# Another written-out order for a 128-row linear layer on one core: rounding before the sum, loads in parts

## The chip, the cores and the metric

One core of a Trainium2 chip runs the kernel. The metric is device time in microseconds (us): the median of the kernel's runs, here 107.94 us from three runs (107.92 to 108.06). A profile of one execution of the kernel before is at hand.

## The reference

```python
x: (4, 1024, 512)   cond_512: (4, 256)   W: (1536, 512)   b: (512,)
hidden = concatenate([cond_512, cond_512], axis=-1)            # (4, 512)
x_mean = mean(x, axis=1, keepdims=True)                        # (4, 1, 512)
fused  = concatenate([x, x_mean * ones, hidden * ones], -1)    # (4, 1024, 1536)
out    = x + relu(einsum('bld,do->blo', fused, W) + b)
```

All in float32. W has three blocks of 512 rows: one for x itself, one for the mean of x over the 1024 places of a batch row, one for `hidden`. The last two give one vector of 512 numbers for each of the four batch rows, called the bias here.

## The kernel before, in words

The output has 32 tiles of 128 places (eight for a batch row), each 128x512. For each tile the core computes x·W by TensorE. To keep float32 accuracy with fast products, x and W are split into a rounded part (`hi`, `w_hi`) and a remainder (`lo`, `w_lo`); a tile needs for each of four blocks j of 128 inputs the three products hi·w_hi, lo·w_hi and hi·w_lo: twelve matmuls of 128x128 by 128x512.

x must be turned (inputs on the partitions) before it can be a stationary operand. The first eight tiles are turned by TensorE (`turn`, L414: four transposes into one PSUM tile `xT`); the other 24 by VectorE from a second, differently laid out load of x called `z` (L416). Tiles 0 to 3 are turned one by one ("whole" pieces: one tile, all four j; pieces 0 to 3), later ones four tiles at a time ("units", one piece for each j: pieces 4 to 7 are tiles 4 to 7, pieces 8 to 11 tiles 8 to 11, and so on). Each piece is rounded by ScalarE (`hi`, L427), and the remainder is taken by VectorE or GpSimd (`lo`, L443). For whole pieces VectorE also sums over the places (`sum`, L436, tile `sums`); in the others ScalarE's accumulator does that. `hi`, `sum` and the VectorE `lo` of a piece read the same PSUM tile, and the program lets a second engine read it only when the first is through, in the order in which they were emitted.

W is split likewise: `w_hi` by ScalarE (L394) or VectorE (L396), `w_lo` by VectorE or GpSimd (L399).

The bias of a row is a chain: GpSimd adds the two halves of the third block of W (`add_cond`, L458, from `w_cond`), ScalarE scales by the condition (`weigh`, L462), GpSimd sums (`term`, L467), ScalarE starts an accumulator (`acc_start`, L478), VectorE adds the mean's four terms (`mean`, L481, from `total` and `scaled`, L471 and L474, and from `w_mean`), then `upper` (ScalarE L487), `fold` (VectorE L491), `rows_hi` (ScalarE L494), `rows_lo` (VectorE L497), one matmul `pb` (TensorE L501) and its copy `bias` (ScalarE L505).

An output tile's PSUM bank is emptied by `freed`: copied by ScalarE (L545) for the first ten tiles, which wait in SBUF for their bias (`biased`, GpSimd L550); added to the bias by VectorE (L547) for others; or, where the bias was put into the bank first (`preload`, ScalarE L517), finished by VectorE in one step (L543). Then come `relu` (ScalarE L553), `finished` (GpSimd L556, adds x) and `stored` (a DMA from SP, L561). Five PSUM banks serve the output tiles, so tile t needs `freed` of tile t-5. There are 13 SBUF output buffers, five of 1 MB for loads of x and W, three for z.

Nothing is left to a scheduler: `make_plan` lists the tasks, and `ORDER`, a string of numbers found offline, says in which order they are emitted. A number's half is the index of the task in `make_plan`, its last bit picks the first or the second engine the task allows. Each engine runs its tasks in that order and waits at each for what it needs; so does SP's queue for the DMA issues. The costs in `make_plan` (MB, ZMB, START and the pairs of numbers) reach the program in one way only: while TensorE would be idle in the first 12 us by these costs, warming matmuls (`fill`, L335) are put in.

Of the kernel before, what the change touches and what calls it, by code (L numbers as in the profile page):

```python
# [8 lines left out]
F32 = mybir.dt.float32  # L9
# [13 lines left out]
HALF = D // 2  # L23
G = 4
S_BUFS, O_BANKS, Z_BUFS, X_BUFS, O_BUFS, N_WARM = 14, 5, 3, 5, 13, 5
BY_PE = (0,1,2,3,4)
PARK = set(range(10))
BIAS_FIRST = {14,15,20,21,22,23,28,29,30,31}
FINE = 4
EXTRA = ()  # L30
XS_BUFS = 4
WARM_TO = 12.0

UNITS = [(0, k, 1) for k in range(4)] + [(0, 4, G)]
# [30 lines left out]
class Plan:  # L65
    HAND = 0.06
    ISSUE, LAND = 1.0, 0.7
    START = {"pe": 3.3, "sp": 0.75, "act": 2.3, "dve": 1.3, "pool": 3.5}

    def __init__(self):  # L70
        self.tasks = {}
# [23 lines left out]
SP = {"sp": (0.42, 0.42)}  # L95
ZQ = {"sp": (0.42, 0.42)}
MB = 2.62
ZMB = 5.4
MM = 0.2335
STEP = 3 * MM  # L100


def x_here(t):
    return ("x", 0, t) if t < G else ("x", t // G, 0)


def due(t, j, n=0, h=0):
    return 6.5 + (t * J + j) * STEP + n * MM + (h or 0) * J * STEP / 2


def make_plan():
    plan = Plan()
    loads = [
        (("x", 0, 0), MB / 4), (("w", 0), MB / 4 + 1.6), (("w", 1), MB / 4), (("x", 0, 1), MB / 4),
        (("w", 2), MB / 4), (("w", 3), MB / 4), (("x", 0, 2), MB / 4), (("x", 0, 3), MB / 4)
    ]
    chain = []
    for key, cost in loads:
        plan.add(key, SP, [], pipe=cost, soft=chain)
        chain = [key]  # L120
    plan.add(("c",), {"act": (0.42, 2.3)}, [], due=-9.0)
    first = chain
    for key in (("w_cond",), ("w_mean",)):
        plan.add(key, SP, [], pipe=MB, soft=first)
    plan.add(("b",), SP, [], pipe=0.05, soft=[("w_cond",)])
    chain = first
    for n, u in enumerate(BY_Z):
        for i in range(NQ):
            deps = []
            if n >= Z_BUFS:  # L130
                deps = [("turn", c) for c in range(len(PIECES)) if PIECES[c][0] == BY_Z[n - Z_BUFS]]
            late = [("hi", 1)] if "act" in ZQ and not n else []
            if "act" in ZQ and n:
                deps.append(("z", BY_Z[n - 1], i))
            plan.add(("z", u, i), ZQ, deps, pipe=ZMB / 4, soft=chain + late)
            chain = [("z", u, i)]
    x_slots = [0, "w", "cond"] + list(range(1, NT // G))
    if 4 in BY_PE:
        x_slots = [0, "w", 1, "cond"] + list(range(2, NT // G))
    chain = first  # L140
    for n, g in enumerate(x_slots):
        if g in (0, "w", "cond"):
            continue
        deps = []
        if n >= X_BUFS:
            v = x_slots[n - X_BUFS]
            deps = ([("w_hi", j) for j in range(J)] + [("w_lo", j) for j in range(J)] if v == "w" else
                    [("add_cond", k) for k in range(KH)] if v == "cond" else
                    [d for i in range(G) for d in x_read(v * G + i)])
        plan.add(("x", g, 0), SP, deps, pipe=MB, soft=chain + ([("w_cond",)] if n > x_slots.index("cond") else []))  # L150
        chain = [("x", g, 0)]
    for j in range(J):
        plan.add(("w_hi", j), {"act": (0.54, 0.63), "dve": (0.35, 0.43)}, [("w", j)])
        plan.add(("w_lo", j), {"dve": (0.61, 0.69), "pool": (1.3, 1.35)}, [("w_hi", j)])

    kinds = {True: [], False: []}
    for c, (u, js) in enumerate(PIECES):
        r, k0, n = UNITS[u]
        whole = len(js) > 1
        deps = ([x_here(t) for t in range(FIRST_TILE[u], FIRST_TILE[u] + n)]  # L160
                if u in BY_PE else [("z", u, i) for i in range(NQ)])
        same = kinds[in_sbuf(c)]
        n_bufs = XS_BUFS if in_sbuf(c) else 2
        if len(same) >= n_bufs:
            deps.append(("lo", same[-n_bufs]))
            if len(PIECES[same[-n_bufs]][1]) > 1:
# [46 lines left out]
    for t in range(NT):  # L213
        r, k = divmod(t, NK)
# [23 lines left out]
    for t in range(NT):  # L238
# [18 lines left out]
        else:  # L257
# [32 lines left out]
def kernel(  # L290
# [67 lines left out]
    def load_x(e, g, i):  # L358
        r, k = divmod(g * G, NK)
        if not i:  # L360
            xs[g] = xpool.tile([P, G, D], F32, tag="x", name=f"x{g}")
        n = 1 if not g else G
        nc.sync.dma_start(out=xs[g][:, i : i + n], in_=xv[r, :, k + i : k + i + n, :])

    def load_z(e, u, i):
# [11 lines left out]
            w_src["x"] = xpool.tile([P, J, D], F32, tag="x", name="w_x")  # L377
        nc.sync.dma_start(out=w_src["x"][:, j, :], in_=Wv[0, :, j])

    def load_cond(e):  # L380
        w_src["cond"] = xpool.tile([P, 2, KH, D], F32, tag="x", name="w_cond")
        nc.sync.dma_start(
            out=w_src["cond"], in_=W[2 * D : 3 * D].rearrange("(s h p) o -> p s h o", p=P, h=KH)
        )

    def load_mean(e):
# [223 lines left out]
```

## Time and profile before

| | |
|---|---|
| median of three runs | 107.94 us (107.92 to 108.06) |
| the profiled execution's own time | 107.55 us |
| its span, first to last instruction | 105.7 us |
| TensorE clock granted | 1.000 |
| PE busy | 100.5 us (95%) |
| VectorE, ScalarE, GpSimd busy | 74.5, 60.1, 71.4 us |
| bytes moved | 26.31 MB, mean 249 GB/s |

All engines' rows are in us from the span's start. PE is TensorE's matmuls, PEld its weight loads, DVE is VectorE, ACT ScalarE, POOL GpSimd, SPq the queue that issues the DMAs. A row's bracket gives how long the engine sat idle before the instruction, and what ended that. Matmuls are pipelined: a row of one matmul shows 0.40 us, though the next begins about 0.23 us after it, so the distance of starts is what counts.

### The profile page before, as it was taken

Reading aid. Unit: us, or ns where it says so; the run is one execution under the profiler, and the core shown is the slowest. Engines: PE = TensorE matmul, PEld = TensorE weight load, DVE = VectorE, ACT = ScalarE, POOL = GpSimd, SP = SyncE. Lnnn points to the kernel's source line nnn. Section 1 sums busy time; section 2 is a strip of 40 time slices with the busy share of each in tenths; the row PEclk is TensorE's granted clock in tenths of the full one; section 3 lists DMA queues with packets and bytes.
Section 4 is the critical chain, followed back from the end, with each engine's and each line's share of the span. In section 5 each row is a group of like instructions: output and inputs, shape, how many; then the busy total and the mean of one; then the engine's idle time right before and its main releaser. Section 6 shows DMA issues by size and latency. Waiting matters only on the chain.

```text
span 105.7 us, 1434 instructions
## 1 busy us (share of the span) xinstructions
PE 100.5 (95%) x448; PEld 78.9 (75%) x448; DVE 74.5 (70%) x109; ACT 60.1 (57%) x134; POOL 71.4 (68%) x64
## 2 busy tenths in 40 slices
PE   5979999999999999999999999999999999999970
PEld 2446877888888788888788788687888888888860
DVE  1287256248999999797999999999989620920160
ACT  5014075997895997779988507799930402970000
POOL 6005080959327499999999999998999980468000
PEclk9999999999999999999999999999999999999999
DMA  2699999999999999999999999318999999727252
GB/s 76 195 370 387 395 418 229 189 199 199 200 199 200 260 177 199 201 201 300 404 397 234 179 243 385 137 58 217 387 411 338 360 260 249 298 109 297 100 207 91
DMA packets 22961, 26.31 MB, mean 249 GB/s; under 512 B 1189, under 2 KB 13737, under 8 KB 22826
## 3 DMA queue, kind: packets, MB, share of 16 engines
q1 hardware_dynamic: 22946, 26.22, 93.0%
q8 instruction: 3, 0.05, 0.2%
q14 instruction: 4, 0.03, 0.1%
q10 hardware_dynamic: 8, 0.00, 0.0%
HBM read 17.83 MB, written 8.39 MB: 248 GB/s over the span
## 4 chain that ended last, share of the span: by engine, by line
PE 93%; DVE 2%; ACT 1%; issue 0%
PE po_None L529 83%; PE xT L414 4%; PE po L529 3%; PE pw L335 2%; PE pb L501 1%; DVE sums L436 1%; DVE lo L443 1%; ACT hi L427 1%; DVE o L543 0%; DVE w_hi L396 0%; DVE warm L323 0%; PE pt L450 0%; DVE one L325 0%
## 5 line engine op out<-in xcount | busy, mean ns | idle before, releaser
L529 PE MATMUL po_None<-w_hi,hi 128*128 128x512 f32 x124 | 48.6, 400 | 0.6 <-DVE w_hi L396 0.6
L529 PE MATMUL po_None<-w_hi,lo 128*128 128x512 f32 x124 | 48.0, 397 | 0.0
L529 PE MATMUL po_None<-w_lo,hi 128*128 128x512 f32 x124 | 47.9, 398 | 0.0
L556 POOL TENSOR_TENSOR o<-o,x 128x512 f32<-128x512 f32 x22 | 27.9, 1300 | 5.6 <-issue 4.5
L529 PEld LDWEIGHTS po_None<-w_hi,hi 128*128 128x128 f32 x124 | 23.2, 188 | 7.2 <-issue 1.1
L529 PEld LDWEIGHTS po_None<-w_lo,hi 128*128 128x128 f32 x124 | 23.2, 188 | 5.7 <-POOL w_lo L399 0.4
L529 PEld LDWEIGHTS po_None<-w_hi,lo 128*128 128x128 f32 x124 | 23.2, 189 | 5.0
L416 DVE STREAM_TRANSPOSE xT<-z 128x512 f32<-128x512 f32 x24 | 25.3, 1094 | 0.1
L427 ACT ACTIVATE hi<-xT 128x512 fp32r<-128x512 f32 x32 | 19.3, 608 | 10.6 <-PE xT L414 5.9
L443 POOL TENSOR_TENSOR lo<-xT,hi 128x512 fp32r<-128x512 f32 x12 | 15.5, 1298 | 4.5 <-ACT hi L427 4.3
L443 DVE TENSOR_TENSOR lo<-xT,hi 128x512 fp32r<-128x512 f32 x20 | 13.4, 683 | 5.2 <-ACT hi L427 5.2
L550 POOL TENSOR_TENSOR o<-o,bias 128x512 f32<-128x512 f32 x10 | 12.9, 1301 | 1.9 <-ACT bias L505 1.9
L553 ACT ACTIVATE o<-o 128x512 f32<-128x512 f32 x22 | 13.1, 622 | 1.3 <-POOL o L550 0.9
L481 DVE SCALAR_TENSOR_TENSOR acc<-w_mean,tot,acc 128x512 f32<-128x512 f32 x16 | 12.1, 753 | 0.9 <-ACT tot L474 0.5
L547 DVE TENSOR_TENSOR o<-po_None,bias 128x512 f32<-128x512 f32 x12 | 7.7, 678 | 5.7 <-ACT bias L505 5.1
L543 DVE SCALAR_TENSOR_TENSOR o<-po_None,x 128x512 f32<-128x512 f32 x9 | 6.1, 687 | 7.3 <-PE po_None L529 7.3
L487 ACT ACTIVATE upper<-acc 64x512 f32<-64x512 f32 x4 | 2.4, 598 | 8.4 <-DVE acc L481 8.4
L467 POOL TENSOR_TENSOR cond<-b_sb,term 128x512 f32<-128x512 f32 x4 | 5.2, 1290 | 2.9 <-ACT term L462 2.9
L436 DVE TENSOR_REDUCE sums<-xT 128x4 f32<-128x512 f32 x4 | 2.7, 691 | 6.2 <-PE xT L414 3.2
L545 ACT ACTIVATE o<-po_None 128x512 f32<-128x512 f32 x10 | 5.5, 602 | 1.6 <-PE po_None L529 1.5
L399 POOL TENSOR_TENSOR w_lo<-w_x,w_hi 128x512 fp32r<-128x512 f32 x1 | 1.6, 1553 | 6.7 <-ACT w_hi L394 6.7
L414 PEld LDWEIGHTS xT<-ident,x 128*128 128x128 f32 x32 | 4.8, 208 | 1.7 <-issue 1.4
(45 smaller groups left out, 72.4 us busy)
## 6 DMA issues: line engine op xcount, KB each, us to landing
out_dram<-o SPq DMA_DIRECT2D x31, 256.0 KB, 4.6
x<-in_x_dram SPq DMA_DIRECT2D x7, 1024.0 KB, 8.6
z<-in_x_dram SPq DMA_DIRECT2D x24, 256.0 KB, 9.3
x<-in_x_dram SPq DMA_DIRECT2D x4, 256.0 KB, 5.7
w_x<-in_L_cond_W_dram SPq DMA_DIRECT2D x4, 256.0 KB, 5.4
w_cond<-in_L_cond_W_dram SPq DMA_DIRECT2D x1, 1024.0 KB, 7.8
w_mean<-in_L_cond_W_dram SPq DMA_DIRECT2D x1, 1024.0 KB, 12.1
out_dram<-o SPq DMA_DIRECT2D x2, 128.0 KB, 2.0
```

The lines of the kernel that those rows point to most:

```text
L414: nc.tensor.transpose(v[:, (m * n + i) * P : (m * n + i + 1) * P], x_t[:, j], ident)
L416: nc.vector.transpose(v[:, : n * P].rearrange("p (n t) -> p n t", t=Q), zs[u].rearrange("p n (a j) -> p n j a", j=J)[:, : n * NQ, js[0], :],)
L427: nc.scalar.activation(hi[c][:, :m], xT[c][:, :m], AF.Copy, accum_out=sums[:, r, js[0], s : s + 1] if len(js) == 1 else None,)
L443: eng[e].tensor_tensor(lo[c][:, :m], xT[c][:, :m], hi[c][:, :m].bitcast(F32), ALU.subtract)
L481: nc.vector.scalar_tensor_tensor(acc[r], w_mean[:, j, :], totals[r][:, j : j + 1], acc[r], ALU.mult, ALU.add)
L529: nc.tensor.matmul(v[:, : m.shape[-1]], lhsT=(hi, lo, hi)[n][p][:, c * P : (c + 1) * P], rhs=m, start=(t not in BIAS_FIRST and i == 1), st ...
L543: nc.vector.scalar_tensor_tensor(o_tile(t)[:, d], v, 0.0, x_tile(t)[:, d], ALU.max, ALU.add)
L545: nc.scalar.activation(o_tile(t), v, AF.Copy)
L547: nc.vector.tensor_tensor(o_tile(t), v, biases[t // NK], ALU.add)
L550: nc.gpsimd.tensor_tensor(outs[t], outs[t], biases[t // NK], ALU.add)
L553: nc.scalar.activation(outs[t], outs[t], AF.Relu)
L556: nc.gpsimd.tensor_tensor(outs[t], outs[t], x_tile(t), ALU.add)
```

## The change

The diff, with the new `ORDER` (as long as the old) left out:

```diff
-BIAS_FIRST = {14,15,20,21,22,23,28,29,30,31}
+BIAS_FIRST = set(range(14,16))|set(range(20,24))|set(range(28,32))     # the same set
+PORTION = {0: 1, 5: 2, 6: 2, 7: 2}
...
-    START = {"pe": 3.3, "sp": 0.75, "act": 2.3, "dve": 1.3, "pool": 3.5}
+    START = {"pe": 3.6, "sp": 0.75, "act": 2.3, "dve": 1.3, "pool": 3.5}
...
+FIRST = [("x", 0, 0), ("w", 0), ("w", 1), ("x", 0, 1), ("w", 2), ("w", 3), ("x", 0, 2), ("x", 0, 3)]
+def portion(g):
+    return PORTION.get(g, G)
 def x_here(t):
-    return ("x", 0, t) if t < G else ("x", t // G, 0)
+    return ("x", t // G, t % G // portion(t // G) * portion(t // G))
...
-    for key in (("w_cond",), ("w_mean",)):
-        plan.add(key, SP, [], pipe=MB, soft=first)
-    plan.add(("b",), SP, [], pipe=0.05, soft=[("w_cond",)])
+    for s in range(2):
+        plan.add(("w_cond", s), SP, [], pipe=MB / 2, soft=[("w_cond", 0)] if s else first)
+    plan.add(("w_mean",), SP, [], pipe=MB + 0.5, soft=first)
+    plan.add(("b",), SP, [], pipe=0.05, soft=[("w_cond", 1)])
...
-        plan.add(("x", g, 0), SP, deps, pipe=MB, soft=chain + ([("w_cond",)] if n > x_slots.index("cond") else []))
-        chain = [("x", g, 0)]
+        for i in range(0, G, portion(g)):
+            plan.add(("x", g, i), SP, deps, pipe=MB * portion(g) / G,
+                     soft=chain + ([("w_cond", 1)] if n > x_slots.index("cond") else []))
+            chain = [("x", g, i)]
...
         if whole:
-            plan.add(("sum", c), {"dve": (0.62, 0.69)}, [("turn", c)])
+            plan.add(("sum", c), {"dve": (0.62, 0.69)}, [("hi", c)])
...
-        plan.add(("add_cond", k), {"pool": (1.27, 1.32)}, [("w_cond",)])
+        plan.add(("add_cond", k), {"pool": (1.27, 1.32)}, [("w_cond", 0), ("w_cond", 1)])
...
 (load_x)
-        n = 1 if not g else G
+        n = portion(g)
         nc.sync.dma_start(out=xs[g][:, i : i + n], in_=xv[r, :, k + i : k + i + n, :])
 (load_cond)
-        nc.sync.dma_start(
-            out=w_src["cond"], in_=W[2 * D : 3 * D].rearrange("(s h p) o -> p s h o", p=P, h=KH)
-        )
+        nc.sync.dma_start(
+            out=w_src["cond"][:, s],
+            in_=W[2 * D + s * H : 2 * D + (s + 1) * H].rearrange("(h p) o -> p h o", p=P),
+        )
```

The other lines of the diff change costs that the planner counts with. The two orders, decoded, begin so on each engine (product t.j.n is tile t, block j, and n = 0, 1, 2 for hi·w_hi, lo·w_hi, hi·w_lo; later products have all three n in one task):

```
before
 PE    turn.0  9 fills  0.0.0 0.0.1 0.1.1 0.1.0 turn.1 0.0.2 0.1.2 0.2.0 0.2.1 1.0.0 1.2.0 1.3.0 0.3.0 1.2.2 ...
 ACT   hi.0 w_hi.2 hi.1 hi.2 hi.3 freed.0 freed.1 hi.4 weigh.0.0 weigh.0.1 weigh.1.0 hi.5 hi.6 acc_start.0 hi.7 ...
 DVE   sum.0 lo.0 w_hi.0 w_hi.1 w_lo.0 w_lo.1 w_hi.3 sum.1 lo.1 w_lo.3 sum.2 sum.3 lo.2 lo.3 cT ...
 POOL  w_lo.2 add_cond.1 add_cond.0 term.0.0 term.0.1 ...
 SP    x.0.0 w.0 w.1 x.0.1 w.2 w.3 x.0.2 x.0.3 w_cond x.1.0 b w_mean z.5 z.6 z.7 x.2.0 z.8 ...
after
 PE    turn.0  8 fills  0.0.0 0.0.1 1 fill 0.0.2 turn.1 0.1.0 0.1.1 0.1.2 0.2.0 0.2.1 1.0.0 1.2.0 1.1.2 1.0.2
       0.2.2 turn.2 1.2.1 turn.3 1.3.0 0.3.1 1.1.1 0.3.0 1.1.0 1.0.1 0.3.2 1.3.2 2.0.0 2.2.2 2.2.0 2.1.0 2.3.0
       turn.4 turn.5 ...
 ACT   hi.0 w_hi.0 w_hi.1 hi.1 w_hi.3 hi.2 hi.3 freed.0 hi.4 hi.5 weigh.0.0 weigh.0.1 hi.6 hi.7 freed.1 scaled.0
       acc_start.0 ...
 DVE   sum.0 lo.0 w_lo.0 w_lo.1 w_hi.2 w_lo.2 sum.1 lo.1 sum.2 lo.3 lo.2 sum.3 lo.4 cT lo.5 lo.6 total.0 lo.7 ...
 POOL  w_lo.3 add_cond.0 add_cond.1 term.0.0 term.0.1 ...
 SP    x.0.0 w.0 w.1 x.0.1 w.2 w.3 x.0.2 x.0.3 x.1.0 w_cond.0 w_cond.1 b w_mean z.5 z.6 x.2.0 z.7 z.8 ...
```

In the order before, `sum` stood ahead of `hi` for piece 0 alone; for pieces 1 to 3 `hi` was ahead already. The first eight loads are issued in the same order in both. The rest of every engine's order, up to the last tile, is a new one too; the numbers of tasks by kind stay as they are, but for three more loads of x, one more of `w_cond`, and two of the four `w_hi` that go from DVE to ACT. The matmul `pb` of rows 0, 1, 2 and 3 stands 10, 6, 6 and 6 matmuls earlier in PE's order than before.

More of the change, by code (lines that the diff above doesn't have):

```diff
@@ L25 @@
 S_BUFS, O_BANKS, Z_BUFS, X_BUFS, O_BUFS, N_WARM = 14, 5, 3, 5, 13, 5
-BY_PE = (0,1,2,3,4)
+BY_PE = (0, 1, 2, 3, 4)
+XEARLY = True
+PORTION = {0: 1, 5: 2, 6: 2, 7: 2}
 PARK = set(range(10))
-BIAS_FIRST = {14,15,20,21,22,23,28,29,30,31}
+BIAS_FIRST = set(range(14,16))|set(range(20,24))|set(range(28,32))
 FINE = 4
@@ L32 @@
 WARM_TO = 12.0
-UNITS = [(0, k, 1) for k in range(4)] + [(0, 4, G)]
+ROW0 = [(0, k, 1) for k in range(4)] + [(0, 4, G)]
+UNITS = list(ROW0)
 UNITS += [(r, k, G) for r in range(1, B) for k in range(0, NK, G)]
@@ L97, with quarters @@
 MB = 2.62
-ZMB = 5.4
+ZMB = 5.28
 MM = 0.2335
 STEP = 3 * MM
+def quarters(u):
+    return [("z", u, i) for i in range(NQ)]
+FIRST = [("x", 0, 0), ("w", 0), ("w", 1), ("x", 0, 1), ("w", 2), ("w", 3), ("x", 0, 2), ("x", 0, 3)]
+def portion(g):
+    return PORTION.get(g, G)
 def x_here(t):
-    return ("x", 0, t) if t < G else ("x", t // G, 0)
+    return ("x", t // G, t % G // portion(t // G) * portion(t // G))
 def due(t, j, n=0, h=0):
@@ L112, in make_plan @@
     plan = Plan()
+    after = {}
     loads = [
-        (("x", 0, 0), MB / 4), (("w", 0), MB / 4 + 1.6), (("w", 1), MB / 4), (("x", 0, 1), MB / 4),
-        (("w", 2), MB / 4), (("w", 3), MB / 4), (("x", 0, 2), MB / 4), (("x", 0, 3), MB / 4)
+        (("x", 0, 0), MB / 4), (("w", 0), MB / 4 + 1.6), (("w", 1), MB / 4 + 0.5), (("w", 2), MB / 4),
+        (("w", 3), MB / 4), (("x", 0, 1), MB / 4), (("x", 0, 2), MB / 4), (("x", 0, 3), MB / 4),
     ]
-    chain = []
+    chain = {}
     for key, cost in loads:
-        plan.add(key, SP, [], pipe=cost, soft=chain)
-        chain = [key]
+        plan.add(key, SP, [], pipe=cost, soft=[chain[key[0]]] if key[0] in chain else [])
+        chain[key[0]] = key
+    for a, c in zip(FIRST, FIRST[1:]):
+        after.setdefault(c, []).append(a)
     plan.add(("c",), {"act": (0.42, 2.3)}, [], due=-9.0)
-    first = chain
-    for key in (("w_cond",), ("w_mean",)):
-        plan.add(key, SP, [], pipe=MB, soft=first)
-    plan.add(("b",), SP, [], pipe=0.05, soft=[("w_cond",)])
+    first = list(chain.values())
+    for s in range(2):
+        plan.add(("w_cond", s), SP, [], pipe=MB / 2, soft=[("w_cond", 0)] if s else first)
+    plan.add(("w_mean",), SP, [], pipe=MB + 0.5, soft=first)
+    plan.add(("b",), SP, [], pipe=0.05, soft=[("w_cond", 1)])
     chain = first
@@ L134, in make_plan @@
                 deps.append(("z", BY_Z[n - 1], i))
-            plan.add(("z", u, i), ZQ, deps, pipe=ZMB / 4, soft=chain + late)
+            plan.add(("z", u, i), ZQ, deps, pipe=ZMB / 4 * UNITS[u][2] / G, soft=chain + late)
             chain = [("z", u, i)]
     x_slots = [0, "w", "cond"] + list(range(1, NT // G))
-    if 4 in BY_PE:
+    if XEARLY:
         x_slots = [0, "w", 1, "cond"] + list(range(2, NT // G))
@@ L149, in make_plan @@
                     [d for i in range(G) for d in x_read(v * G + i)])
-        plan.add(("x", g, 0), SP, deps, pipe=MB, soft=chain + ([("w_cond",)] if n > x_slots.index("cond") else []))
-        chain = [("x", g, 0)]
+        for i in range(0, G, portion(g)):
+            plan.add(("x", g, i), SP, deps, pipe=MB * portion(g) / G,
+                     soft=chain + ([("w_cond", 1)] if n > x_slots.index("cond") else []))
+            chain = [("x", g, i)]
     for j in range(J):
-        plan.add(("w_hi", j), {"act": (0.54, 0.63), "dve": (0.35, 0.43)}, [("w", j)])
+        plan.add(("w_hi", j), {"act": (0.54, 0.63), "dve": (0.37, 0.43)}, [("w", j)])
         plan.add(("w_lo", j), {"dve": (0.61, 0.69), "pool": (1.3, 1.35)}, [("w_hi", j)])
@@ L159, in make_plan @@
         whole = len(js) > 1
+        w = n * len(js)
         deps = ([x_here(t) for t in range(FIRST_TILE[u], FIRST_TILE[u] + n)]
@@ L168, in make_plan @@
         same.append(c)
-        plan.add(("turn", c), {"pe": (0.5, 0.7)} if u in BY_PE else {"dve": (1.0, 1.09)}, deps,
+        plan.add(("turn", c), {"pe": (0.125 * w, 0.125 * w + 0.2)} if u in BY_PE else {"dve": (0.1 + 0.225 * n, 0.19 + 0.225 * n)}, deps,
                  soft=[("turn", c - 1)] if c else [])
@@ L174, in make_plan @@
             deps += [d for i in range(UNITS[v][2]) for j in js_v for d in made(FIRST_TILE[v] + i, j)]
-        a = 0.52 if whole else 0.7
+        a = (0.52 if whole else 0.7) - 0.055 * (4 - w)
         plan.add(("hi", c), {"act": (a, a + 0.09)}, deps, soft=[("hi", c - 1)] if c else [])
-        plan.add(("lo", c), {"pool": (1.27, 1.32)} if in_sbuf(c) else {"dve": (0.61, 0.69)}, [("hi", c)])
+        plan.add(("lo", c), {"pool": (0.1 + 0.2925 * w, 0.15 + 0.2925 * w)} if in_sbuf(c) else {"dve": (0.13 + 0.12 * w, 0.21 + 0.12 * w)}, [("hi", c)])
         if whole:
-            plan.add(("sum", c), {"dve": (0.62, 0.69)}, [("turn", c)])
+            plan.add(("sum", c), {"dve": (0.62, 0.69)}, [("hi", c)])
     plan.add(("cT_pe",), {"pe": (0.15, 0.3)}, [("c",)], soft=made(0, J - 1))
@@ L262, in make_plan @@
         plan.add(("stored", t), SP, [("finished", t)], pipe=MB / 4, due=due(t + (17 if t in PARK else 7), J))
+    for key, keys in after.items():
+        plan.tasks[key][4].extend(k for k in keys if k not in plan.tasks[key][4])
     return plan
 ORDER = """
[19 rows of a table removed]
[19 rows of a table added]
 """
@@ L378, in load_w, with load_cond @@
         nc.sync.dma_start(out=w_src["x"][:, j, :], in_=Wv[0, :, j])
-    def load_cond(e):
-        w_src["cond"] = xpool.tile([P, 2, KH, D], F32, tag="x", name="w_cond")
+    def load_cond(e, s):
+        if not s:
+            w_src["cond"] = xpool.tile([P, 2, KH, D], F32, tag="x", name="w_cond")
         nc.sync.dma_start(
-            out=w_src["cond"], in_=W[2 * D : 3 * D].rearrange("(s h p) o -> p s h o", p=P, h=KH)
+            out=w_src["cond"][:, s],
+            in_=W[2 * D + s * H : 2 * D + (s + 1) * H].rearrange("(h p) o -> p h o", p=P),
         )
```

38 rows, old and new, of the table ORDER are left out of this document.

## The prediction

> **What bounds the kernel now.** I read the page first, then the chain of waits, then TensorE alone, then the other engines' rows in the first 30 us.
>
> ```profile
> span 105.7 us, 1434 instructions
> ...
> PE 100.5 (95%) x448; PEld 78.9 (75%) x448; DVE 74.5 (70%) x109; ACT 60.1 (57%) x134; POOL 71.4 (68%) x64
> ...
> DVE  1287256248999999797999999999989620920160
> ...
> POOL 6005080959327499999999999998999980468000
> ...
> GB/s 76 195 370 387 395 418 229 189 199 199 200 199 200 260 177 199 201 201 300 404 397 234 179 243 385 137 58 217 387 411 338 360 260 249 298 109 297 100 207 91
> ```
>
> TensorE is busy 95% of the span; DVE and POOL come near full only between a quarter and four fifths of it. The chain shows whether those ever hold TensorE up.
>
> ```profile
> 4.45 0.70 DVE sums L436
> ...
> 5.81 0.69 DVE lo L443
> ...
> 6.98 1.16 PE po_None L529 x4
> ...
> 13.21 0.95 PE xT L414 x8
> ...
> 21.97 12.82 PE po_None L529 x55
> 34.79 0.23 PE pb L501
> ...
> 48.33 0.23 PE pb L501
> ...
> 66.77 0.23 PE pb L501
> ...
> 102.50 0.42 DVE o L543
> ```
>
> Before 6.98 the chain goes through VectorE's sum, the remainder (between them ScalarE's rounding, at 5.18, shown below) and W's rounding; from there it stays on PE to the last `freed` (102.50). Later products cost 12.82/55 = 0.233 us each, a transpose 0.95/8 = 0.119. Now what PE does between the first product and the end, as stages (the columns are length, PE busy and count, clock, DMA share, GB/s):
>
> ```profile
> 6.98:16.34 9.36, 9.23 (x44) 1.00 1.04 399
> 16.34:21.73 5.39, 5.39 (x32) 1.00 1.17 185
> 21.73:102.46 80.73, 80.73 (x358) 1.00 0.96 245
> ```
>
> And of the products alone:
>
> ```profile
> 6.98:16.34 9.36, 8.15 (x29) 1.00 1.04 399
> ```
>
> From 16.34 on PE is busy in every 0.01 us, so nothing is to be had there but by starting it earlier. In 6.98 to 16.34 stand 29 products, twelve transposes (tiles 1 to 3) and the two small ones of the condition (0.21 by the distance of their start to the next): 29 x 0.233 + 12 x 0.119 + 0.21 = 8.40 of 9.36 us. So 0.96 us are lost there to waits too short to show as busy gaps, and the wait before 6.98 can be shortened. That is all that this change can win. The tail after the last product stays as it is.
>
> **The change, part by part.** The times below are of one execution: span 105.7, own time 107.55, so 1.85 around it; the median of the runs is 107.94, 0.39 above. I forecast a difference and take it from the median.
>
> *Rounding before the sum.* Only piece 0 changes.
>
> ```profile
> 5.18 0.60 ACT L427 ACTIVATE hi<-xT 128x512 fp32r<-128x512 f32 x1 [2.95 <-DVE sums L436]
> 8.28 0.63 ACT L394 ACTIVATE w_hi<-w_x 128x512 fp32r<-128x512 f32 x1 [2.51 <-DMA w_x<-in_L_cond_W_dram]
> ```
>
> ScalarE waited 2.95 us for `sums`, which had PSUM from 4.45. Now hi.0 runs 4.45 to 5.05 and sum.0 after it; DVE starts follow each other by about 0.60:
>
> ```profile
> 8.97 0.43 DVE L396 CAST w_hi<-w_x 128x512 fp32r<-128x512 f32 x1 [0.57 <-DMA w_x<-in_L_cond_W_dram]
> 9.44 0.69 DVE L436 TENSOR_REDUCE sums<-xT 128x4 f32<-128x512 f32 x1
> 10.04 0.68 DVE L443 TENSOR_TENSOR lo<-xT,hi 128x512 fp32r<-128x512 f32 x1
> ...
> 24.05 3.13 DVE L481 SCALAR_TENSOR_TENSOR acc<-w_mean,tot,acc 128x512 f32<-128x512 f32 x4 [0.54 <-ACT tot L474]
> 27.09 1.10 DVE L416 STREAM_TRANSPOSE xT<-z 128x512 f32<-128x512 f32 x1
> ...
> 33.02 0.68 DVE L497 TENSOR_TENSOR rows<-acc,rows 64x512 fp32r<-64x512 f32 x1
> ```
>
> (0.60 from 9.44 to 10.04.) So sum.0 5.07, lo.0 5.68 to 6.37, w_lo.0 6.28 to 6.97. The remainder itself wins only 0.13 us: the sum is now between. The gain is that ScalarE is free for w_hi.0 at 5.05. When is w.0 there?
>
> ```profile
> 1.18 0.89 SPq L378 DMA_DIRECT2D w_x<-in_L_cond_W_dram  x2
> 2.11 0.43 SPq L363 DMA_DIRECT2D x<-in_x_dram  x1
> ...
> 5.18 0.38 SPq L382 DMA_DIRECT2D w_cond<-in_L_cond_W_dram  x1
> 6.77 0.38 SPq L363 DMA_DIRECT2D x<-in_x_dram  x1
> ```
>
> ```profile
> DMA to landing us min/median/max: 4.0/5.4/5.9
> ```
>
> w.0 was issued at 1.18 and landed after 4.0 (the least of the four): 5.18, when SP went on with `w_cond`. `x.1.0` went out at 6.77, which I read as w.1's landing. So w_hi.0 is 5.18 to 5.81 (0.63, the row at 8.28), w_hi.1 6.77 to 7.40.
>
> *PE's opening.* These fills precede product 0.0.0:
>
> ```profile
> 4.25 2.11 PE L335 MATMUL pw<-warm 128*128 128x512 bf16 x9
> ...
> 10.61 0.50 PE L529 MATMUL po_None<-w_lo,hi 128*128 128x512 f32 x1
> ...
> 13.92 0.71 PE L529 MATMUL po_None<-w_hi,lo 128*128 128x512 f32 x2
> 14.56 0.28 PE L450 MATMUL pt<-ident,c_sb 4*128 4x4 f32 x2
> ```
>
> Nine fills end at 6.36; 2.11/9 = 0.23 for each, so eight end near 6.13. Product 0.0.0 is then at about 6.0 to 6.13, not 6.98. 0.0.1 waits for lo.0: 6.40. One fill, to 6.86. 0.0.2 waits for w_lo.0: 7.00. turn.1 from 7.23 (x.0.1 went out at 2.11; the loads of 256 KB take 5.7 us in the median, quoted below, so 7.4 to 7.8: 0.2 to 0.6 us late, of which 0.30 would only shorten the wait for w_hi.2 that follows; I take none, by the run before, where its transposes went at 7.98 behind other work without a wait). 0.1.0 7.73, 0.1.1 7.96, 0.1.2 8.20. 0.2.0 needs w_hi.2, and w.2 landed at 8.28 (ScalarE's row): cast on DVE 8.28 to 8.71 (0.43, the row at 8.97), so 8.73. Then 0.2.1 8.97, 1.0.0 9.20 (hi.1 is done at 8.6), 1.2.0, 1.1.2, 1.0.2, and 0.2.2, the thirteenth product, at 10.13. In the trace the thirteenth stood at 10.61, with the same twelve products and turn.1 done before it. Ahead by 0.48.
>
> From there the new order has work ready: lo.1 (DVE: sum.1 9.28, lo.1 to 10.57) for 1.2.1 at 10.85; w_hi.3 (w.3 landed by 8.97) to 9.6 and w_lo.3 on POOL to about 11.2 for 0.3.2 at about 13; hi.2 11.7 for 2.0.0 at 13.4; lo.2 13.5 before turn.4 takes its PSUM tile at 14.6. By 10.61 the old order had lost 3.63 - 12 x 0.233 - 4 x 0.119 = 0.36, so 0.60 of the 0.96 came later: 0.17 around the condition's transposes (13.92 + 2 x 0.233 = 14.39, start 14.56), which stay, and 0.43 which go (the largest before 16.34, where turn.4 stood behind lo.2). Gain 0.48 + 0.43 = 0.91 us.
>
> *x.1.0 ahead of w_cond, w_cond in two.*
>
> ```profile
> x<-in_x_dram SPq DMA_DIRECT2D x7, 1024.0 KB, 8.6
> ...
> x<-in_x_dram SPq DMA_DIRECT2D x4, 256.0 KB, 5.7
> ...
> w_cond<-in_L_cond_W_dram SPq DMA_DIRECT2D x1, 1024.0 KB, 7.8
> w_mean<-in_L_cond_W_dram SPq DMA_DIRECT2D x1, 1024.0 KB, 12.1
> ```
>
> x.1.0 takes the issue at 5.18 and, like `w_cond` there, 7.8 us: 13.0, wanted at 14.6, so it hides. The halves of `w_cond` take the places at 6.77 and after: with x.1.0's 8.6, 15.5 instead of 13.0. This lies on the bias chain:
>
> ```profile
> 13.07 2.53 POOL L458 TENSOR_TENSOR wc<-w_cond 128x512 f32<-128x512 f32 x2 [2.52 <-DMA w_cond<-in_L_cond_W_dram]
> ```
>
> add_cond 15.5 to 18.1 (2.53), term.0.0 and term.0.1 as long again (the same operation and shape), 20.7; acc_start.0 0.6, 21.4. The other input, row 0's total, comes earlier, since turn.4 to turn.7 do: turn.7 18.3 to 18.9, hi.7 20.0, scaled.0 20.8. So mean.0 starts at 21.4, not 24.05, though `w_cond` is 2.5 us later. It ends at 24.5; turn.8 1.10, fold.0, three more turns, rows_lo.0 at 29.9. pb.0 is wanted ten matmuls (2.33) and 0.91 earlier than 34.79: 31.55. Cover 1.6 us. The price with no cover: PE stands still for what is missing.
>
> *The extra DMAs.* Four more issues of about 0.4 us on SP. z.5 and all behind it move back by one or two; x.2.0 goes past z.7 (z.7 later by 1 MB at the page's 200 GB/s of that stretch, some 5 us; its turn.16 is due at 42 by the steps below). x.5 to x.7 in parts sit in SP's queue among the stores and feed tiles from 20 on. The price lies between a small gain (the first part lands earlier) and a late part, under which `freed` of its tile holds a PSUM bank and PE. I take nothing: the second part's bytes come when the whole's did, and the cover is whatever held PE without a gap from 21.73 on.
>
> A rule speaks against the parts. The Trainium skill, "DMA: Bandwidth & Descriptors", section "Rules for kernel authors", advises 1 MiB or more for each transfer; "Bandwidth" puts 1 MB at 341 GB/s and 64 KB at 138. If halves ran at 138, an estimate from that page, `w_cond` would be 4.9 us late (7.6 against 2.7) and the kernel some 2.4 us slower. The trace disagrees: while the first 256 KB loads ran (5.3 to 10.6 us) the page's slices show 370 and 387 GB/s, so by rows it is nothing.
>
> *The rest of the order.* Every product after 21.7 must be fed 0.91 us earlier. I followed the two tight places by hand with the rows' durations (ACT 0.6, POOL 1.3, DVE 0.6 or 1.05). pb.1 stands six matmuls earlier: 48.33 - 1.40 - 0.91 = 46.0. bias.0 32.4; four `freed` on ACT, hi.12 to hi.15 36.9; total.1, relu.0, scaled.1, relu.4, acc_start.1 38.7; mean.1 to 41.8; upper.1 stands behind freed.8, that is behind tile 8's last product at about 41.9: 43.1; fold.1, turn.17, rows_lo.1: 45.5. Cover 0.5. pb.2: 66.77 - 1.40 - 0.91 = 64.5; by the same steps rows_lo.2 is done at 63.3. Cover 1.2. DVE and POOL, the full engines of the middle, have row 0's mean 2.6 us earlier and PE only 0.91, so their cover grows rather than shrinks.
>
> **The sum.** 107.55 - 0.91 = 106.64 for a profiled execution, 107.94 - 0.91 = 107.03 for the median. I say 107.0.
>
> **The rivals.**
> (1) *Forecast*: 0.6 to 1.3 us faster, 106.65 to 107.35. The upper end takes all 0.96 and the 0.85 of the earlier first product, less the fill (0.23) and the wait for w.2 (0.30); the lower end has x.0.1 at its latest (0.3 left over).
> (2) *Half is given back in the middle.* upper.1 behind freed.8 is the place: each 0.1 us over the cover of 0.5 costs 0.1. With 0.5 lost: 107.5. For it: the cover is an end of fifteen added steps. Against: the old trace has the same kind of margin everywhere (rows_lo.0 ends 33.70, pb.0 34.79) and lost nothing.
> (3) *It does nothing.* The first eight loads have the old order, so if landings bound the opening (w.1 at 6.77, w.2 at 8.28, w.3 at 8.97 are the same), an earlier first product only waits longer. That would show as waits for w_x and x in the opening that add to 0.9. Against: thirteen products are ready by 10.4 by those very landings. Time 107.9.
> (4) *Slower: w_cond's last half is late.* `w_mean`, issued at 7.65 into the same queue, took 12.1 us. Were that the half's, it would land at 7.3 + 12.1 = 19.4, 3.9 after 15.5; less the cover of 1.6 pb.0 holds PE for 2.3: 107.94 - 0.91 + 2.3 = 109.3. It decides from a landing after 18.0. Against: `w_mean` is behind it in the queue, and x.1.0, in that place, took 8.6 to 8.9. The Trainium skill's rule above would act in this way.
>
> **How the numbers follow.** (1) 0.62, (2) 0.17, (3) 0.09, (4) and its like 0.12. A difference under 0.2% (0.22 us) can't be told from none. Faster: (1) and (2), 0.78 after a little of (2) falls within; within: 0.10; slower: 0.12. The range 106.6 to 107.9 holds (1), (2) and most of (3), and leaves out (4) and a gain over 1.3. The likeliest case's own range is 106.65 to 107.35.
>
> **What would show it.** In the trace after: ScalarE's hi.0 at 4.45 released by PE, `sums` at 5.07; first product at 6.0 to 6.13; one wait of about 0.3 us before 8.73 for w_hi; turn.4 at 14.6, not 16.34; add_cond at 15.5; mean.0 at 21.4; pb at about 31.5, 46, 64.5 with no idle PE before; the last `freed` at 101.6. I am wrong if PE idles over 0.3 us after 17 (rival 2 or 4), or if the opening's waits for loads sum to 0.9 more than here (rival 3).

## The result and the profile after

The changed kernel takes 106.71 us in the median of four runs (106.36 to 106.93), against 107.94 (107.92 to 108.06) for the kernel before beside it. One of the four runs of the kernel before took 114.71 us, in a slower state of the chip, and is left out, as such runs are in every median and ratio below. The ratio is 0.9885 [0.9861, 0.9909]: faster by 1.15%, 1.2 us. The forecast was 107.0, its own range 106.65 to 107.35. The profiled execution of the changed kernel took 106.93, 0.2 above its median, and that of before 107.55, 0.4 below its own; so the two traces differ by only 0.62 us. A second profile of the changed kernel (the first experiment below) took 106.49 and is used beside the first.

Lines moved by 23 to 25 in the listing: products are L554 (before L529), transposes L439 (L414), fills L358 (L335). The page and its chain, after:

```profile
span 105.1 us, 1449 instructions
...
PE 100.9 (96%) x448; PEld 79.6 (76%) x448; DVE 73.7 (70%) x107; ACT 61.3 (58%) x136; POOL 71.2 (68%) x64
...
4.57 2.85 PE pw L358 x8
...
19.75 12.61 PE po_None L554 x54
32.36 0.23 PE pb L526
...
46.83 0.23 PE pb L526
...
65.25 0.23 PE pb L526
...
102.17 0.42 DVE o L568
```

The chain no longer passes through VectorE's sum, remainder and rounding of W. It runs on the fills, and they end late: by the rows of PE eight took 3.06 us, where nine took 2.11 before. PE alone, after:

```profile
4.37 3.06 PE L358 MATMUL pw<-warm 128*128 128x512 bf16 x8
7.08 0.58 PE L554 MATMUL po_None<-w_hi,hi 128*128 128x512 f32 x1
...
8.19 0.64 PE L439 MATMUL xT<-ident,x 128*128 128x128 f32 x4
...
9.43 0.50 PE L554 MATMUL po_None<-w_hi,hi 128*128 128x512 f32 x1
...
10.46 0.86 PE L554 MATMUL po_None<-w_lo,hi 128*128 128x512 f32 x3
...
15.39 1.12 PE L439 MATMUL xT<-ident,x 128*128 128x128 f32 x8
```

The first product is at 7.08, even later than before (6.98). The thirteenth is the third of the row at 10.46: 10.93, 0.32 behind the 10.61 of before. What follows is faster: turn.4 stands at 15.39 and no longer behind lo.2. How full PE is in that stage, and in two microseconds ahead of it (length, PE busy and count, clock, DMA share, GB/s):

```profile
4.40:5.40 1.00, 1.00 (x4) 1.00 0.57 143
5.40:6.40 1.00, 1.00 (x4) 1.00 0.89 279
```

```profile
7.08:15.39 8.31, 8.31 (x43) 1.00 1.05 384
```

In 7.08 to 15.39 stand 27 products, one fill and twelve transposes (the row counts 43, as three more reach across its ends): 28 x 0.233 + 12 x 0.119 = 7.95 of 8.31, so 0.36 us of short waits where before had 0.96. Of these, 0.34 lie ahead of the thirteenth product (3.85 us from the first to it, for twelve products, turn.1 and the fill, 3.51), and only 0.02 behind it. The two rows of 4.40 to 6.40 hold only six matmuls in 2 us (two of them are counted in both), though the clock column shows 1.00: matmuls start 0.43 apart there and about 0.23 apart later. The column does not show this early half rate; the distances of the starts do.

VectorE and ScalarE in the opening, after (two views of one engine each):

```profile
4.61 0.60 ACT L452 ACTIVATE hi<-xT 128x512 fp32r<-128x512 f32 x1 [2.38 <-PE xT L439]
5.32 0.63 ACT L419 ACTIVATE w_hi<-w_x 128x512 fp32r<-128x512 f32 x1
6.81 0.63 ACT L419 ACTIVATE w_hi<-w_x 128x512 fp32r<-128x512 f32 x1 [0.86 <-DMA w_x<-in_L_cond_W_dram]
```

```profile
5.24 0.69 DVE L461 TENSOR_REDUCE sums<-xT 128x4 f32<-128x512 f32 x1 [3.96 <-ACT hi L452]
...
8.94 0.43 DVE L421 CAST w_hi<-w_x 128x512 fp32r<-128x512 f32 x1 [0.78 <-DMA w_x<-in_L_cond_W_dram]
...
22.37 3.13 DVE L506 SCALAR_TENSOR_TENSOR acc<-w_mean,tot,acc 128x512 f32<-128x512 f32 x4 [0.56 <-ACT acc L503]
26.45 1.11 DVE L441 STREAM_TRANSPOSE xT<-z 128x512 f32<-128x512 f32 x1 [0.96 <-DMA z<-in_x_dram]
...
31.14 0.69 DVE L522 TENSOR_TENSOR rows<-acc,rows 64x512 fp32r<-64x512 f32 x1
```

hi.0 is released by PE and `sums` by hi.0, as the change intends, and W's first rounded block is ready at 5.95 instead of just before 6.98. It only waited: PE was still in its fills. GpSimd's `add_cond`, after:

```profile
16.50 2.55 POOL L483 TENSOR_TENSOR wc<-w_cond 128x512 f32<-128x512 f32 x2 [4.86 <-DMA w_cond<-in_L_cond_W_dram]
```

Two more differences lie where the prediction expected none. First, at 68 us. In the window 60 to 75 of the kernel before, weight loads by form and PE's rows show:

```profile
L529 PEld LDWEIGHTS po_None<-w_hi,hi 128*128 128x128 f32 x21 | 4.0, 188 | 1.2 <-ACT po_None L517 0.4
```

```profile
68.01 0.40 PE L529 MATMUL po_None<-w_lo,hi 128*128 128x512 f32 x1
68.33 0.50 PE L529 MATMUL po_None<-w_hi,hi 128*128 128x512 f32 x1
68.66 0.40 PE L529 MATMUL po_None<-w_hi,lo 128*128 128x512 f32 x1
```

Two distances of 0.32 and 0.33 where 0.233 is normal: a weight load waited for ScalarE's `preload` of the bank, and PE's busy time shows nothing of it, since a matmul's row is 0.40 long. That is 0.19 us. The same view of after has no such releaser:

```profile
L554 PEld LDWEIGHTS po_None<-w_hi,hi 128*128 128x128 f32 x22 | 4.1, 188 | 1.0
```

Second, the end. SP's last wait, before and then after (total, times, longest):

```profile
SPq L606 <- DMA out_dram<-o: 1.4, 1, 1.4
```

```profile
SPq L631 <- DMA out_dram<-o: 1.0, 1, 1.0
```

From the end of the last `freed` to the end of the span: before 105.7 - 102.92 = 2.8, after 105.1 - 102.59 = 2.5 us.

The two traces then add up: -0.32 in the opening, +0.41 from there to turn.4 and the condition's transposes (0.60 of short waits before; after, 0.02 and the 0.17 at the condition, which stays), +0.24 later (102.50 - 102.17 = 0.33, less 0.41 - 0.32 = 0.09), +0.27 in the tail: 0.60 of 0.62.

### The profile page after: what moved, and what is told of

It is laid out like the page before. It is cut to its first block, busy times and chain, and to the rows that moved or that the text cites. A ratio compares the mean times of both kernels' runs of the same rounds, so it can differ in the third digit from the quotient of the medians.

```text
span 105.1 us, 1449 instructions
## 1 busy us (share of the span) xinstructions
PE 100.9 (96%) x448; PEld 79.6 (76%) x448; DVE 73.7 (70%) x107; ACT 61.3 (58%) x136; POOL 71.2 (68%) x64
## 4 chain that ended last, share of the span: by engine, by line
PE 96%; DVE 1%; issue 0%
PE po_None L554 83%; PE pw L358 5%; PE xT L439 4%; PE po L554 3%; PE pb L526 1%; DVE o L568 0%; DVE warm L346 0%; PE pt L475 0%; DVE one L348 0%
## 5 line engine op out<-in xcount | busy, mean ns | idle before, releaser
L554 PE MATMUL po_None<-w_hi,hi 128*128 128x512 f32 x124 | 48.8, 400 | 0.0
L554 PE MATMUL po_None<-w_hi,lo 128*128 128x512 f32 x124 | 48.7, 397 | 0.0
L554 PE MATMUL po_None<-w_lo,hi 128*128 128x512 f32 x124 | 48.4, 398 | 0.0
L554 PEld LDWEIGHTS po_None<-w_hi,hi 128*128 128x128 f32 x124 | 23.3, 188 | 5.8 <-DVE w_hi L421 0.3
L554 PEld LDWEIGHTS po_None<-w_lo,hi 128*128 128x128 f32 x124 | 23.3, 188 | 5.5
L554 PEld LDWEIGHTS po_None<-w_hi,lo 128*128 128x128 f32 x124 | 23.3, 188 | 5.2
L468 POOL TENSOR_TENSOR lo<-xT,hi 128x512 fp32r<-128x512 f32 x12 | 15.5, 1313 | 2.4 <-ACT hi L452 2.3
L530 ACT ACTIVATE bias<-pb 128x512 f32<-128x512 f32 x4 | 2.4, 600 | 9.1 <-PE pb L526 9.1
L358 PE MATMUL pw<-warm 128*128 128x512 bf16 x14 | 5.8, 569 | 1.2 <-DVE one L348 1.2
L487 ACT ACTIVATE term<-wc,cT 128x512 f32<-128x512 f32 x8 | 5.5, 717 | 1.0 <-POOL wc L483 1.0
```

The costliest lines, as they stand in the source:

```text
L358: nc.tensor.matmul(pw, lhsT=warm[:, :P], rhs=warm, start=True, stop=True)
L468: eng[e].tensor_tensor(lo[c][:, :m], xT[c][:, :m], hi[c][:, :m].bitcast(F32), ALU.subtract)
L554: nc.tensor.matmul(v[:, : m.shape[-1]], lhsT=(hi, lo, hi)[n][p][:, c * P : (c + 1) * P], rhs=m, start=(t not in BIAS_FIRST and i == 1), st ...
```

## The experiments

Each is built on the kernel before or after. Orders are shown decoded. Ratios are to the kernel before, run on the same chip. Wherever fills are fixed as numbers, they are those of the base kernel if nothing else is said.

**The changed kernel once more**, as the mark for the others.

```diff
-            if s < WARM_TO and s - pe_free > 0.35: ...      # fills by the planner's costs
+            for _ in range({0.0.0: 8, 0.0.2: 1}.get(key, 0))   # the same nine, as numbers
```

> The changed kernel as it is, a second profile of it. In the first one the eight warming matmuls came 0.43 us apart until 6.5 us and the first product stood at 7.08 (the kernel before: 0.23 apart, 6.98). Theory clock: when TensorE's rate doubles differs from run to run, so here the distance may be 0.21 from the start; then the first product is at 6.0 to 6.2 and the span 104.5 to 104.8; if it is 0.43 again, 7.0 to 7.2 and 105.1. Rival: the eight are slow for a reason that lies in the new order, so 0.43 again whenever it runs. Ratio to before 0.985 to 0.992 by both.

106.83 us (105.98 to 107.12), ratio 0.9892 [0.9859, 0.9925]. Its profile, 106.49:

```profile
4.26 2.91 PE L359 MATMUL pw<-warm 128*128 128x512 bf16 x8
6.83 0.58 PE L555 MATMUL po_None<-w_hi,hi 128*128 128x512 f32 x1
...
7.95 0.64 PE L440 MATMUL xT<-ident,x 128*128 128x128 f32 x4
...
10.04 0.87 PE L555 MATMUL po_None<-w_lo,hi 128*128 128x512 f32 x3
```

The thirteenth product is at 10.51: 0.10 ahead of before, where the other execution was 0.32 behind. Between the two, the half rate of the start ended at 6.3 us instead of 6.7 (read from the distances of the fills). turn.4 stands at 14.96 here, the last `freed` at 101.73, and the span is 104.7.

**Rounding before the sum, alone** (in the kernel before).

```diff
 emission:  turn.0 ...
-  sum.0 hi.0
+  hi.0 sum.0
```

> The kernel before with one thing changed: piece 0 is rounded ahead of its sum, all else in the old order. Theory rounding-frees-ScalarE: alone it is worth nothing (within 0.15 us), since lo.0 still comes after hi.0 and the sum (5.8 us) and W's first rounding still stands on VectorE behind lo.0, so the first product stays at 6.9 to 7.0. Rival (the rounding is the first link, so the whole chain moves up): first product at 6.3, 0.5 to 0.7 us faster.

107.73 us, 0.9984 [0.9964, 1.0004]. hi.0 starts at 4.77, released by PE, but W's first rounding is still on VectorE behind the sum and the remainder, at 6.61:

```profile
7.17 0.47 PE L530 MATMUL po_None<-w_hi,hi 128*128 128x512 f32 x1 [0.23 <-DVE w_hi L397]
```

The swap by itself is worth nothing that can be told from none.

**The sum first again** (in the kernel after).

```diff
-plan.add(("sum", c), {"dve": (0.62, 0.69)}, [("hi", c)])
+plan.add(("sum", c), {"dve": (0.62, 0.69)}, [("turn", c)])
 emission:
-  hi.0 ... sum.0
+  sum.0 hi.0 ...
```

> The changed kernel with piece 0's sum ahead of its rounding again, all else in the new order. Theory: hi.0 and w_hi.0 come 0.6 to 0.7 us later (w_hi.0 done near 6.6), lo.0 and w_lo.0 hardly later; 0.2.0 still waits for w.2, so the time is within 0.3 us of the changed kernel (0 to 0.3 slower). Rival (the swap carries the gain): 0.6 to 1.0 us slower than the changed kernel, near the kernel before.

106.92 us, 0.991 [0.9877, 0.9943]: not told apart from the changed kernel. w_hi.0, at 5.98 now, still hides under the fills (first product 7.12).

**w_cond ahead of x.1.0 again** (in the kernel after).

```diff
 SP:  x.0.3
-  x.1.0 w_cond.0 w_cond.1
+  w_cond.0 w_cond.1 x.1.0
```

> The changed kernel with both parts of w_cond issued ahead of x.1.0 again, all else in the new order. Theory loads: x.1.0 lands near 16 to 17 us, TensorE stands at turn.4, which the new order wants at 15.4, for 0.6 to 1.6 us, and the time grows by that; add_cond starts near 14. Rival (x.1.0's place is hidden anyway): within 0.3 us of the changed kernel.

107.89 us, 1.0003 [0.9979, 1.0027]: the whole gain is gone. GpSimd had its `w_cond` at 13.65 instead of 16.50, which brought nothing; PE waited for x.1.0:

```profile
14.71 0.86 PE L555 MATMUL po_None<-w_hi,hi 128*128 128x512 f32 x3
16.33 1.21 PE L440 MATMUL xT<-ident,x 128*128 128x128 f32 x8 [0.76 <-DMA x<-in_x_dram]
```

Start to start 16.33 - 14.71 = 1.62, for three products of 0.70: 0.92 lost.

**x.1.0 ahead of w_cond, alone** (in the kernel before).

```diff
 SP:  x.0.3
-  w_cond x.1.0
+  x.1.0 w_cond
```

> The kernel before with x.1.0 issued ahead of w_cond, all else in the old order. Theory (the load's place pays only with the new order of the engines): turn.4 still stands behind lo.2 at 16.3, and w_cond comes 2.5 to 3 us later to a ScalarE order that has three weigh steps ahead of hi.5, so the bias chain of row 0 is late and pb.0 holds TensorE: 0.3 to 2 us slower than before. Rival (the load is the gain by itself): 0.5 us or more faster.

108.75 us, 1.0066 [1.0046, 1.0085]: slower. turn.4 stood at 17.16 there, behind lo.2 as before, so the early load brought nothing. I had counted on `pb` holding PE; no such wait is in the trace. The loss lies in the opening, in

```profile
9.78 0.50 PE L530 MATMUL po_None<-w_hi,hi 128*128 128x512 f32 x1 [0.23 <-ACT w_hi L395]
```

(w.2 landed late), in the first product, which stood at 7.32 instead of 6.98 because the half rate lasted longer in that execution, and in a distance of 0.49 instead of 0.23 from the product at 21.97 to turn.7, which waited for its PSUM tile: lo.5 was late, because ScalarE's hi.5 stood behind `weigh`, which waited for the later `w_cond`. How much of the 0.7 us each has was not settled. What it shows: the early load pays only with an order of PE that wants it.

**No parts** (in the kernel after).

```diff
-PORTION = {0: 1, 5: 2, 6: 2, 7: 2}
+PORTION = {0: 1}
-    for s in range(2):
-        plan.add(("w_cond", s), SP, [], pipe=MB / 2, ...)
+    plan.add(("w_cond",), SP, [], pipe=MB, soft=first)
```

> The changed kernel with w_cond and the last three x groups loaded whole, all else as changed. Theory: the parts are worth nothing, 106.6 to 107.0 us; add_cond starts within 0.5 us of 15.9 to 16.5. Rival (whole loads land later and hold the bias chain or a bank): 0.3 us or more slower, with TensorE idle before pb or after 67 us. Other rival (fewer issues, as the rule on 1 MB loads has it): 0.2 us or more faster.

107.20 us, 0.9938 [0.9914, 0.9962]: about 0.4 slower than with the parts, though the interval still touches that of the changed kernel's repeat. The parts do not show on PE: first product 7.36, last `freed` 102.27, which is 94.91 us, against 101.73 - 6.83 = 94.90 with parts in the repeat (95.09 in the first execution); `add_cond` began at 16.16. The late first product is that execution's half rate, which lasted to 7.3. What the trace shows besides is the tail, 105.5 - 102.69 = 2.8, with SP's last wait as in the kernel before:

```profile
SPq L628 <- DMA out_dram<-o: 1.4, 1, 1.4
```

**New opening, old rest; old opening, new rest.** Both up to product 4.0, everything else on all engines from the other order. The old opening has the sum ahead of the rounding and the nine fills, as in the kernel before, and `w_cond` in its two parts.

```diff
-  <after's order>
+  <after's up to product 4.0> + <before's, less what is done>
```

> The changed kernel's order up to tile 4's first product, then the old order for what is left. Theory opening: the gain is made before 17 us and the rest has cover, so within 0.3 us of the changed kernel: 106.5 to 107.1. Rival (the new rest is needed for an earlier TensorE): the old rest makes TensorE wait before pb or a bank and 0.4 us or more are given back.

111.73 us, 1.0371 [1.0346, 1.0396]: 4 us slower, and my expectation that the old rest has cover fell. In the new opening x.2.0 goes past z.7. In the old rest, turn.16, which reads z.7, stands on VectorE ahead of row 1's `total` and `mean`. VectorE, then PE, then PE's stages:

```profile
41.63 1.13 DVE L442 STREAM_TRANSPOSE xT<-z 128x512 f32<-128x512 f32 x1 [2.70 <-DMA z<-in_x_dram]
```

```profile
50.28 0.80 PE L527 MATMUL pb<-rows,ones 128*128 128x512 f32 x1 [2.09 <-DVE rows L523]
50.87 0.63 PE L555 MATMUL po_None<-w_hi,hi 128*128 128x512 f32 x1
51.30 0.63 PE L555 MATMUL po_None<-w_hi,lo 128*128 128x512 f32 x1
```

```profile
47.50:50.50 3.00, 0.91 (x4) 0.94 1.14 317
50.50:53.50 3.00, 3.00 (x8) 0.50 1.02 382
53.50:60.00 6.50, 6.50 (x29) 1.00 0.98 265
```

One late load held `pb` by 2.09 us, and afterwards PE ran at half rate (products 0.43 apart, clock 0.50) until 53.4. The wait and the half rate together make 3.8 of the 4.0 us by which the last `freed` is later than in the changed kernel (106.20 against 102.17). In the new order turn.16 stands behind mean.1, which is why the later z.7 costs nothing there.

```diff
-  <after's order>
+  <before's up to product 4.0> + <after's, less what is done>
```

> The old order up to tile 4's first product (sum first, w_cond's parts ahead of x.1.0, 9 fills), then the new order. Theory opening: no faster than the kernel before, 107.6 to 108.3, slower where pb, which the new order has 6 to 10 matmuls earlier, finds its bias chain late: TensorE idle before pb by up to 2 us, so up to 109.5. Rival (the middle or the tail carries the gain): 107.2 or less.

107.47 us, 0.9973 [0.9956, 0.999]: 0.3 us faster than before. By its own trace (an execution 0.6 above the median) `pb` never waits and the tail is the short one; what it lacks against the changed kernel, 0.9 us, would then be the opening with the new load order.

**Four fills instead of nine** (in the kernel after), and **none**.

```diff
-FILLS = {0.0.0: 8, 0.0.2: 1}
+FILLS = {0.0.0: 4}          # the other: {}
```

> The changed kernel with 4 warming matmuls ahead of the first product, not 8, and none before product 0.0.2. Theory clock: the matmul rate doubles 4.1 to 7.1 us from the start, another time in each run, and eight slow ones hold the first product until 6.8 to 7.3; with four it stands at 6.0 to 6.3 and the time falls by 0.2 to 0.4 us (106.4 to 106.6), less where w.2 lands late. Rival (the fills are what brings the rate up): with TensorE less busy the doubling comes 1 to 3 us later and the products before it take 0.43, so 0.3 to 1.0 us slower.

106.58 us (106.22 to 106.86), 0.9884 [0.9862, 0.9907]: the lowest median of all, 0.25 under the changed kernel beside the first experiments, though the intervals overlap, so that this stays open.

```profile
5.87 0.76 PE L555 MATMUL po_None<-w_hi,hi 128*128 128x512 f32 x1
...
7.82 0.75 PE L440 MATMUL xT<-ident,x 128*128 128x128 f32 x4
...
10.04 0.87 PE L555 MATMUL po_None<-w_lo,hi 128*128 128x512 f32 x3
```

The first product is 0.96 earlier than in the repeat of the changed kernel, turn.1 only 0.13, and the thirteenth is at the same 10.51. This turn.1 waited for x.0.1, as its weight load shows:

```profile
7.82 0.56 PEld L440 LDWEIGHTS xT<-ident,x 128*128 128x128 f32 x4 [0.36 <-DMA x<-in_x_dram]
```

So an earlier first product is not what the opening hangs on.

> The changed kernel without any warming matmul after the first five. Theory landing: the opening is bounded by w_hi.0 at 5.9, x.0.1 near 7.7 and w.2 near 8.3 to 8.9, so it takes no harm as long as the rate has doubled by 8: 106.4 to 106.9. Rival (the fills keep the rate): TensorE idle from 4.6 to 5.9 and from 6.4 on delays the doubling to 9 us or later, products until then 0.43 apart, 0.5 to 1.5 us slower than the changed kernel.

108.03 us, 0.9997 [0.9968, 1.0026]: over 1 us slower than the changed kernel. The half rate lasts to 10.8:

```profile
9.54 0.63 PE L555 MATMUL po_None<-w_lo,hi 128*128 128x512 f32 x1
9.96 0.63 PE L555 MATMUL po_None<-w_hi,hi 128*128 128x512 f32 x1
10.39 0.63 PE L555 MATMUL po_None<-w_hi,lo 128*128 128x512 f32 x1
```

**Four more DMAs, in both kernels**, to see whether the tail hangs on their number: SP issues 75 before, 79 after.

```diff
+        if key == ("stored", 24):
+            for i in range(4):
+                spare = const.tile([1, 16], F32, name=f"spare{i}")
+                nc.sync.dma_start(out=spare, in_=b.rearrange("(o d) -> o d", o=1)[:, :16])
```

> The kernel before with four loads of 64 B into unused tiles issued ahead of tile 24's store, so that it issues as many DMAs as the changed kernel. From TensorE's last product to the end of the span the kernel before takes 3.2 to 3.3 us, the changed one 3.0, and with whole loads again 3.25 with the same TensorE stream. Theory count: where the last store falls among the DMAs' completion semaphores sets this, so here it is 3.0 and the time 0.2 to 0.3 us less than before. Rival (the new order or the smaller x loads drain sooner): 3.2 to 3.3, no change.

107.44 us, 0.9961 [0.9942, 0.9979]: four useless loads of 64 bytes make the kernel before 0.4 us faster. Last `freed` at 102.41, span 105.4: a tail of 105.4 - 102.83 = 2.6 instead of 2.8, so the tail accounts for more than half of it; the rest was not placed.

> The changed kernel with the same four small loads. Theory count: the last store falls where it fell before the change, so the tail is 3.2 to 3.3 us and the time 0.2 to 0.3 us more than the changed kernel. Rival: 3.0, no change.

107.02 us, 0.9913 [0.9895, 0.9932]: 0.2 above the changed kernel's repeat, which the times alone do not tell from none; the tail is 105.0 - 102.17 = 2.8. SP's last wait, and PE's rows where the fills ended early by chance:

```profile
SPq L635 <- DMA out_dram<-o: 1.4, 1, 1.4
```

```profile
6.28 0.58 PE L555 MATMUL po_None<-w_hi,hi 128*128 128x512 f32 x1
...
7.84 0.75 PE L440 MATMUL xT<-ident,x 128*128 128x128 f32 x4 [0.17 <-DMA x<-in_x_dram]
```

So the last wait is the long one (1.4) with 75 DMAs in both kernels and with 83 in the changed one, and the short one (1.0 to 1.1) with 79 in both, in all fourteen traces of this case. That the number decides among these three is shown; why it does (which of a set of counters the last store falls on would fit) is only argued.

## Why the prediction was right, point by point

The sign and the size came out (0.91 forecast, 1.2 measured), but the terms did not all hold. The 0.43 before turn.4 was foreseen for the right reason; the 0.48 of the opening did not come, and two terms that I had put at nothing, 0.19 and 0.27, made up for it. That the sum came out so near is partly luck.

- *The first product at 6.0 to 6.13, the thirteenth at 10.13: 0.48.* This term failed. It was measured at +0.10 in one execution and -0.32 in another. Two steps of it are wrong. "0.23 for each" fill was the price of one execution, whose half rate ended at 4.1; after, it ended at 6.7 and 6.3, and eight fills took 3.06 and 2.91. And "I take none" for x.0.1: where the fills did end early (first product 6.28 and 5.87), turn.1 waited to 7.84 and 7.82, 0.6 after my 7.23, and the thirteenth product stood no earlier than 10.5. That is 0.4 of the 0.48 even in a lucky execution. Rival 3, landings bound the opening, was right about this stage where the fills ended early; where they ended late, the fills themselves bound it for the most part. About the rest it was wrong. (The twelve products ahead of the thirteenth are not the same in the two orders, as I wrote: before has 1.3.0 and 0.3.0 there, after 1.1.2 and 1.0.2. They take the same time, so the comparison stands.)
- *The short waits before turn.4 go: 0.43.* Held: 0.41, and 0.42 in the repeat. From the thirteenth product to turn.4 it took 4.46 and 4.45 us, forecast 14.6 - 10.13 = 4.47; turn.4 stood at 15.39 and 14.96 instead of 14.6 only because the thirteenth product was late. w_cond first again takes the whole gain away, so it hangs on x.1.0 being there for the earlier turn.4 and on the order of PE that uses it; the load alone, in the old order, is slower.
- *Rounding before the sum.* The rows came as said (4.61, 5.24, 5.32 against 4.45, 5.07, 5.18), and the step is worth nothing by itself or in reverse: the fills cover it.
- *w_cond's halves at 15.5, mean.0 at 21.4, pb at 31.5, 46 and 64.5 with no idle PE.* `add_cond` began at 16.50 and mean.0 at 22.37, each about 1 us late; `pb` at 32.36, 46.83, 65.25, without a wait. The covers held, though the one of pb.0 was smaller than I had summed: rows_lo.0 ended at 31.83, 0.5 ahead of `pb` and not 1.6, after VectorE had waited 0.96 for z at 26.45. For pb.1 and pb.2 they were 0.5 and 1.15, forecast 0.5 and 1.2. Rival 4 needed a landing after 18.0, and rival 2 a wait at `pb`; neither came. But the cover belongs to the new order: with the old rest, z.7 was late by 2.70 and PE stood 2.09, just the mechanism of the slower rival with another load.
- *"From 16.34 on ... nothing is to be had there".* Wrong by 0.19: two waits at 68 us, hidden since PE's row counts as busy to the end of a matmul. I had seen through the same thing for 6.98 to 16.34 by counting products, and did not count the rest of the span. The new rest removes them: the traces with the old rest show them, those with the new rest do not.
- *"The tail after the last product stays as it is", and "I take nothing" for the extra DMAs.* Wrong by 0.27, on the good side. The parts change nothing on PE (94.91 and 94.90 us from first product to last `freed`); four more DMAs shorten the last wait, whatever they load. The Trainium skill, "DMA: Bandwidth & Descriptors", section "Rules for kernel authors", advises 1 MiB or more for each transfer; in these runs the halves cost PE nothing, so for this kernel the measurement decides against the rule. The estimate of 4.9 us in the prediction took the rate given for 64 KB for halves of 512 KB, so it was a worst case.

For the changed kernel's repeat the sum is 0.10 + 0.42 + 0.25 + 0.27 = 1.04, of 107.55 - 106.49 = 1.06; the 0.25 is (102.50 - 101.73) - 0.10 - 0.42, the 0.19 at 68 and 0.06 that I did not place. The medians differ by 1.2, and an execution of before at its own median was not profiled.

## What to carry to other kernels

A load that is moved up and the order of the engine that wants it are one change: either alone was at best nothing here, and an opening with another kernel's rest cost 4 us. Count matmuls against the time of every stage, not only of the one in question, since short waits do not show in a busy share. And a price from the first microseconds of one execution is a range: look for what comes next (here a load's landing) before an earlier start is credited.

## What the hardware showed that I had not expected

The half rate of TensorE at the start ended between 4.1 us (the kernel before) and 7.3 us (without parts) with fills of the same kind in front, and at 6.7 and 6.3 us in two executions of the changed kernel. The Trainium skill, "TensorE: Matmul & The Clock Gate", section "What's actually happening", says that the moment varies by 500 ns either way, as the gate's window runs freely; that it varies these traces show too, but by 3 us. The same section of the Trainium skill speaks of an idle window of about 3.4 us before the rate drops; with the new opening and the old rest 2.09 us of idle PE was enough, and the half rate then lasted from about 50.3 to 53.4. And the wait at the end hangs on how many DMAs were issued, 1.4 us with 75 or 83 against 1.0 to 1.1 with 79, whatever the added ones carried.
